# Moving closing stores, closing loads and context loads from the head of a pair to its middle in a two-layer graph kernel

## The chip, the cores and the metric

The kernel runs on one core of a Trainium2 chip. The metric is the device time of one execution in microseconds (us). A kernel is timed in several runs, and the median is taken. Besides, one execution is recorded by the hardware profiler; its page and its trace are what the readings below are taken from.

## The reference

There are 8 batches of 2048 nodes with 256 features, and one adjacency matrix. Layer 0 is a four-head attention whose softmax runs within chunks of 256 keys; layer 1 is a graph attention over all neighbours. Each has a residual sum and a layer norm. Cut to what matters:

```
# layer 0: chunked attention, then output, residual, norm
scores = einsum('bhnd,bhjcd->bhnjc', q, kc) / sqrt(64)
scores = where(mask == 0, -10, clip(scores, -10, 10))
ctx    = einsum('bhnjc,bhjcd->bhnd', softmax(scores, -1), vc)
out    = LN(ctx @ Wo.T + bo + x) * gamma + beta
x1     = LN(x + out)
# layer 1: e_ij = leaky_relu(s_src_i + s_dst_j) on the edges
Wh     = (x1 @ W).reshape(..., 4, 64)
h      = einsum('bijh,bjhd->bihd', softmax(where(adj, e, -inf), 2), Wh)
return LN(x1 + elu(h))
```

## The kernel before

All is float32. For each batch `b` the kernel runs layer 0 of `b` together with layer 1 of batch `b - 1`, and in the same loop it *closes* batch `b - 2`: it adds x1 to layer 1's result, takes the last layer norm and stores the output.

Layer 0 of a batch is a loop over 32 *pairs* (variable `p`). The queries are cut in four *quarters* `q` of 512; a quarter has 8 pairs, numbered `i` from 0 to 7: four for the first two heads and four for the other two. A pair holds two slots, `s0` and `s1`; a slot is one chunk of 256 keys for two heads. In a pair, in the order in which the code issues it:

- the head: stores that wait in a list are sent (`send`), the mask tile of the pair after the next is loaded (`load_slab`, tile `slab`), and other loads are issued; then VectorE's steps of the table `FIRST_OF` and the turn of a context tile;
- `burst(p + 1)`: the four score products (`ps`, 64 by 512, line L400) of the next pair, each evicted by VectorE with clip and mask (L417) into `pr`, and put through the exponential by ScalarE (L440). PSUM has three double banks for them, so the fourth product waits for the first eviction;
- layer 1's part: `make` builds a tile `e` on VectorE (L859) from a row (`srow`) and an edge tile (`et`), `use` multiplies it on TensorE (`pa`, L888). A pair makes and uses four tiles: two are made before the middle of the pair, two after it. Each `make` loads the edge tile that is wanted three tiles later (L805), from four buffers, so that load waits for an earlier `e`;
- the middle: VectorE's steps of `MIDDLE_OF` and `NEXT_MIDDLE`, steps of the closing, and then `product(s0)` (`pc`, L451): the slot's probabilities by the values;
- the rest: the other evictions and exponentials, more of layer 1, and `product(s1)`; at the end the steps on ScalarE, among them the closing's `finish`, which scales the output tile (L566, tile `x1g`) and puts its store (L969) on the list.

All this is an order written out by hand: every engine works through its instructions in the order of the code, and so does SP, which issues nearly all of the DMAs. An instruction of SP that waits holds those behind it.

The queries' buffer `qT` is used again for the context. When two heads of a quarter are done, ScalarE's queue stores the context to DRAM (`ctxD`, L484); `load_context` reads it back in four DMAs of 64 KB with blocks of 32 by 32 placed for the turn (L282), and `turn_context` turns it on VectorE (L495, 128 by 512) into `qT`. The output product (`po`, L602) of a quarter runs in pairs 2 and 3 of the next. The object `Between` carries a quarter from there to x1: `bias` (L586) and `shift` (L590) add the output's bias and the norm's beta to the residual `xg`, 128 by 1024.

The closing of batch `b - 2` follows the table `CLOSING`: for each pair the group of 512 nodes and the step. `load` reads x1 of a group from DRAM (L960, 512 KB), `add` adds it to layer 1's result (L963, VectorE), `sums` and `squares` run on ScalarE, `factors` on VectorE and GpSimd, `finish` as above. Batches 0 and 1 have nothing to close.

Of the kernel before, what the change touches and what calls it, by code (L numbers as in the profile page):

```python
# [21 lines left out]
def adj_resnorm_kernel(  # L22
# [47 lines left out]
    QP = QS // 2  # L70
# [134 lines left out]
    def send():  # L205
        while outgoing:
            outgoing.pop(0)()
# [285 lines left out]
    def turn_context(q, hp):  # L493

        nc.vector.transpose(qT[:, hp, q * CH : (q + 1) * CH], sums.pop((q, hp))[:, 0, :])  # L495
# [79 lines left out]
    class Between:  # L575
# [86 lines left out]
    FIRST_OF = {  # L662
        3: lambda o: o.add((0, 1)),
        4: lambda o: o.add((2, 3)),
        6: lambda o: o.shift(),
    }
    MIDDLE_OF = {
        1: lambda o: o.bias(),
        6: lambda o: o.a.factors(),
        7: lambda o: o.scale(),  # L670
    }
# [376 lines left out]
    for g in range(NCH):  # L1048
# [21 lines left out]
            finish_constants()  # L1070

    CLOSING = {
        -1: [(0, "load", HOME), (1, "load", HOME), (2, "load", HOME_Y), (3, "load", HOME_Y)],
        0: [(0, "add"), (0, "sums")],
        1: [(2, "add"), (0, "squares")],
        2: [(0, "factors"), (0, "finish")],
        3: [(1, "add"), (1, "sums")],
        4: [(1, "squares")],
        5: [(1, "factors"), (1, "finish")],
        6: [(2, "sums")],  # L1080
        7: [(3, "add"), (2, "squares")],
# [32 lines left out]
    for b in range(B):  # L1114
        waug = blocks.tile([P, NT, H, D1], F32, tag="waug", name="waug")
        sd = small.tile([P, 2 * H, NT], F32, tag="sd", name="sd", bufs=1)
        closing = Closing(b - 2, CLOSING) if b > 1 else None
        if closing:
            closing.do(-1, "load")
        group = before = None  # L1120
        for p in range(PAIRS):
            s0, s1 = 2 * p, 2 * p + 1
            q, i = p // QP, p % QP
            along = lower if b + 1 < B or s0 < SLOTS - LATE else None
            more = p + 1 < PAIRS

            def hook(now, later):
                if group and i in now:
                    now[i](group)
                if before and i in later:  # L1130
                    later[i](before)

            send()
            if p + 2 < PAIRS:
                load_slab(p + 2)
            if i == 0 and q:
                before, group = group, Between(b, q - 1, sd, waug)
            if closing:
                closing.do(p, "load")
            if i == 1 and q:  # L1140
                load_context(b, q - 1, 1)
            if i == QP // 2 + 1:
                load_context(b, q, 0)
            if p == PAIRS - 2 and b + 1 < B:
                turns = [project(b + 1, g) for g in range(NCH)]
                turns[0].pop(0)()

            hook(FIRST_OF, {})
            if i == QP - 1:
                turn_context(q, 0)  # L1150
            if p:
                normalize(s0 - 1)
            if more:
                us = units_of(p + 1)
                waiting = burst(p + 1)
                evict(*waiting[0][0], waiting[0][1])
                exps(*us[0])
                exps(*us[1])
            if along:
                along.rest(1)  # L1160
                along.make()
                along.use()
                along.make()
            else:
                if more:
                    evict(*waiting[1][0], waiting[1][1])
                    exps(*us[2])
                if not lower and masks.left():
                    masks.step()
            hook(MIDDLE_OF, NEXT_MIDDLE)  # L1170
            if closing:
                closing.do(p, "add", "factors")
            if i == 2 and q:
                turn_context(q - 1, 1)
            product(s0)
            if along:
                normalize(s0)
                if more:
                    for us_ps in waiting[1:]:
                        evict(*us_ps[0], us_ps[1])  # L1180
            elif more:
                evict(*waiting[2][0], waiting[2][1])
                exps(*us[3])
            if i == 0 and q:
                send_context(b, q - 1, 1)
            if i == QP // 2:
                send_context(b, q, 0)
            if along:
                if more:
                    exps(*us[2])  # L1190
                along.rest(1)
                along.use()
                along.make()
                along.use()
                along.make()
                along.use()
            else:
                normalize(s0)
                if not lower and masks.left() and (p < QP - 2 or p % 2 == 0):
                    masks.step()  # L1200
            if p == PAIRS - 1:
                if b + 1 < B:
                    turns[0].pop(0)()
                group.again()
            product(s1)
            if along and more:
                exps(*us[3])
            hook(LAST_OF, NEXT_LAST)
            hook(FINALLY_OF, NEXT_FINALLY)
            if closing:  # L1210
                closing.do(p, "sums", "squares", "finish")
        normalize(SLOTS - 1)

        send()
        before = group
        gd, fs = factors(b, sd, waug)
        group = None

        def begin():
            nonlocal group  # L1220
            group = Between(b, NCH - 1, sd, waug)

        def ctx():
            context(NCH - 1, 1)

        coming = Layer1(b, gd, waug)
        spare.clear()

        parts = WHOLE if b + 1 < B else HALVES

        def start_next():
            for us, ps in burst(0):
                evict(*us, ps)

        early = [
            lambda: before.b2.stats(every),
            lambda: None,
            lambda: before.finish(),
            lambda: before.load(ep.tile([P, KC, CH], F32, tag="e", name="x1t") if b + 1 < B else None),
            lambda: before.turn(),  # L1240
            lambda: before.values((0, 1), parts),
            lambda: before.values((2, 3), parts),
        ]

        steps = [
            lambda: group.bias(),
            lambda: group.output(every, parts),
            lambda: group.add(every),
            lambda: (group.shift(), group.a.stats(every)),
            lambda: group.a.apply(group.y),  # L1250
            lambda: (group.scale(), group.again(), group.b2.stats(every)),
            lambda: group.finish(),
            lambda: group.turn_all(),
            lambda: group.values((0, 1), parts),
            lambda: group.values((2, 3), parts),
        ]
        if b + 1 < B:
            (k0, v0, q0), (l1, t1, k1, v1, q1), (l2, t2, k2, v2, q2), (l3, t3, k3, v3, q3) = turns
            rest = [lambda: lower.rest(1)] if lower else []
            order = [begin, early[0], *rest, l1, k0, ctx, early[2], v0, steps[0], *rest, steps[1], t1, l2, *rest]  # L1260
            order += [q0, steps[2], early[3], steps[3], l3, k1, *rest, steps[4], v1, early[4], t2, q1]
            order += [steps[5], k2, steps[6], early[5], early[6], steps[7], coming.begin, v2, t3]
            order += [lambda: [load_slab(p) for p in range(2)], steps[8], steps[9]]
            order += [lambda: k3(fs[0]), fs[1], lambda: q2(fs[2]), coming.start, v3, start_next]
            order += [lambda: [exps(*us) for us in units_of(0)], q3, coming.make, coming.make]
        else:

            step = lower.step
            order = [begin, early[0], lambda: coming.load_half(0, 0), step, ctx, early[1], step, steps[0], steps[1], early[2], step]
            order += [steps[2], step, steps[3], early[3], step, steps[4], step, steps[5], early[4], step]  # L1270
            order += [steps[6], early[5], step, steps[7], early[6], step, steps[8], step, steps[9], step]
            order += [fs[0], step, fs[1], step, fs[2], coming.start]
            order += [step] * 5
            assert sum(p is step for p in order) == LATE
        for piece in order:
            send()
            piece()
        send()
        undone = lower.tail if lower else []
        lower = coming  # L1280
        if b + 1 == B:
            lower.begin()
        lower.tail += undone
# [57 lines left out]
```

## Time and profile before

| | |
|---|---|
| median of the three timed runs | 3684.75 us (3678.33 to 3687.97) |
| the profiled execution | 3676.19 us |
| its span, first to last instruction | 3674.4 us |
| granted TensorE clock, mean | 0.991 |
| DMA traffic | 512.33 MB, 139 GB/s |
| eviction L417 (128 x 1024), mean of one | 1205 ns, 960 of them |
| `e` L859 (128 x 1024), mean of one | 1335 ns, 896 of them |
| closing store L969, `out_dram<-x1g` | 24, 512 KB each, 3.3 us from issue to landing |
| x1 load L960, `x1g<-x1D` | 24, 512 KB each, 6.1 us to landing |
| context load L282, `ctx<-ctxD` | 224, 64 KB each, 3.8 us to landing |
| mask tile L388 and edge tile L805 | 256 and 896, 256 KB each, 4.2 and 3.3 us to landing |

Busy times on the page are unions of the instructions' times, with the share of the span. In a row of a timeline stand the start, the time from the first instruction's start to the last one's end, the engine, the line, the operation and tiles, how many were merged, and in brackets the idle time before it with what ended it. PE is TensorE's matrix products, PEld its weight loads, SPq the queue of SP. In the list of waits a row has the total in us, the number of times and the longest. "Issue" is idle time in which the engine waited for nothing that the profile shows.

### The profile page before, as it was taken

How to read it: one execution, taken by the hardware profiler on the slowest of the kernel's cores; microseconds unless marked ns; L12 is line 12 of the kernel's file. 1: busy time of each engine (PE TensorE's matmuls, PEld its weight loads, DVE VectorE, ACT ScalarE, POOL GpSimd, SP SyncE). 2: the span in 40 equal slices, each digit the busy share in tenths (PEclk: the TensorE clock that was granted, in tenths of full speed). 3: DMA queues.
4: the chain of work that ended last, by engine and by line, in shares of the span. 5: the costliest groups of instructions: out<-in, count | busy, mean ns of one | idle time of the engine just before them, and what ended most of it. 6: DMA issues, size and time to landing. Idle time of an engine off the chain costs nothing. (4 is left out here: it accounts for less than half of the span.)

```text
span 3674.4 us, 169302 instructions
## 1 busy us (share of the span) xinstructions
PE 3529.9 (96%) x76884; PEld 2627.9 (72%) x76884; DVE 3043.1 (83%) x3652; ACT 2302.7 (63%) x4119; POOL 1437.2 (39%) x1259
## 2 busy tenths in 40 slices
PE   8999999999999999999999999999999999998777
PEld 5666677777777677776777767777677776775677
DVE  5886689968899698995999959998789977896787
ACT  5786556656666566665666656665566655666376
POOL 1555333333333333333433424334234333334376
PEclk9999999999999999999999999999999999999898
DMA  7754344545555455554555545555455554543432
GB/s 192 174 131 94 109 141 144 147 116 159 153 143 145 101 166 152 149 149 116 149 152 144 136 135 163 146 149 125 135 152 149 152 125 143 152 144 94 142 129 83
DMA packets 692866, 512.33 MB, mean 139 GB/s; under 512 B 429616, under 2 KB 528304, under 8 KB 692144
## 3 DMA queue, kind: packets, MB, share of 16 engines
q1 hardware_dynamic: 642144, 467.80, 46.0%
q10 hardware_dynamic: 50000, 33.70, 2.9%
q8 instruction: 601, 9.85, 1.1%
q14 instruction: 121, 0.99, 0.1%
HBM read 440.27 MB, written 61.08 MB: 136 GB/s over the span
## 5 line engine op out<-in xcount | busy, mean ns | idle before, releaser
L440 ACT ACTIVATE pr<-pr 128x1024 f32<-128x1024 f32 x960 | 997.8, 1054 | 445.3 <-DVE pr L417 371.9
L417 DVE SCALAR_TENSOR_TENSOR pr<-ps,slab 128x1024 f32<-128x1024 f32 x960 | 1117.5, 1205 | 118.3 <-PE ps L400 95.3
L859 DVE SCALAR_TENSOR_TENSOR e<-srow,gd,et 128x1024 f32<-128x1024 f32 x896 | 1168.3, 1335 | 25.3 <-PE pa L888 9.5
L888 PEld LDWEIGHTS pa<-waug,e 128*64 128x64 f32 x32768 | 1015.1, 140 | 233.3 <-issue 184.5
L888 PE MATMUL pa<-waug,e 128*64 128x65 f32 x32768 | 1069.2, 225 | 54.7 <-DVE e L859 30.6
L451 PE MATMUL pc<-vaug,pr 128*64 128x65 f32 x30720 | 989.4, 222 | 35.5 <-issue 25.4
L451 PEld LDWEIGHTS pc<-vaug,pr 128*64 128x64 f32 x30720 | 943.2, 138 | 57.6 <-issue 29.1
L475 POOL TENSOR_TENSOR part<-raw,rd 128x512 f32<-128x512 f32 x448 | 477.5, 1066 | 1282.3 <-DVE rd L468 1277.9
L400 PE MATMUL ps<-qT,kT 64*64 64x512 f32 x8192 | 950.3, 597 | 14.3 <-DVE pr L417 13.2
L458 ACT COPY raw<-pc 128x520 f32<-128x520 f32 x512 | 302.6, 591 | 553.2 <-PE pc L451 550.7
L400 PEld LDWEIGHTS ps<-qT,kT 64*64 64x64 f32 x8192 | 289.4, 132 | 497.4 <-issue 272.7
L477 POOL TENSOR_TENSOR acc<-acc,part 128x512 f32<-128x512 f32 x448 | 587.1, 1311 | 35.2
L468 DVE RECIPROCAL rd<-raw 128x8 f32<-128x8 f32 x512 | 100.7, 197 | 176.8 <-ACT raw L458 167.7
L475 POOL TENSOR_TENSOR acc<-raw,rd 128x512 f32<-128x512 f32 x64 | 66.8, 1043 | 362.2 <-DVE rd L468 362.2
L644 PE MATMUL pw<-w_sb,x1T 128*64 128x264 f32 (+1 forms) x800 | 124.7, 391 | 4.8 <-DVE x1T L300 4.7
L344 PE MATMUL pp<-xT,wk_sb 128*128 128x512 f32 x256 | 118.4, 602 | 2.9 <-DVE xT L300 1.6
L602 PE MATMUL po<-wo_sb,qT 128*64 128x256 f32 (+1 forms) x912 | 120.2, 379 | 0.0
L344 PE MATMUL pp<-xT,wq_sb 128*128 128x512 f32 x256 | 117.4, 598 | 0.0
L924 ACT ACTIVATE sums<-sums,dn 128x64 f32<-128x64 f32 x448 | 117.1, 334 | 0.4 <-ACT y L566 0.4
L360 PE MATMUL pv<-wv_sb,xT 128*128 128x256 f32 x512 | 116.6, 381 | 0.0
L360 PEld LDWEIGHTS pv<-wv_sb,xT 128*128 128x128 f32 x512 | 95.9, 190 | 20.2 <-issue 7.2
L830 POOL TENSOR_TENSOR e<-e,et 128x1024 f32<-128x1024 f32 x42 | 90.0, 2146 | 48.4 <-ACT e L829 41.1
(140 smaller groups left out, 2525.1 us busy)
## 6 DMA issues: line engine op xcount, KB each, us to landing
et<-edgeD SPq DMA_DIRECT2D x896, 256.0 KB, 3.3
slab<-clipD SPq DMA_DIRECT2D x256, 256.0 KB, 4.2
srow<-rowD SPq DMA_DIRECT2D x64, 512.0 KB, 4.9
xg<-in_x_dram SPq DMA_DIRECT2D x32, 512.0 KB, 5.4
x1D<-y ACTq DMA_DIRECT2D x32, 512.0 KB, 2.9
ctxD<-acc ACTq DMA_DIRECT2D x56, 256.0 KB, 3.7
ctx<-ctxD SPq DMA_DIRECT2D x224, 64.0 KB, 3.8
xp<-in_x_dram SPq DMA_DIRECT2D x224, 64.0 KB, 2.4
```

The costliest lines, as they stand in the source:

```text
L344: nc.tensor.matmul(pps[c], lhsT=w[:, kc, c * P : (c + 1) * P], rhs=st["xT"][:, kc, :], start=(kc == 0), stop=(kc == KC - 1),)
L360: nc.tensor.matmul(pv[:, u, :], lhsT=st["xT"][:, kc, u * P : (u + 1) * P], rhs=wv_sb[:, kc, :], start=(kc == 0), stop=(kc == KC - 1),)
L400: nc.tensor.matmul(ps[z * D : (z + 1) * D, k, :], lhsT=kT[rows, hp, t * P + z * D : t * P + (z + 1) * D], rhs=qT[rows, hp, cols], start=Tr ...
L417: nc.vector.scalar_tensor_tensor(pr, ps, -CLIP, row.unsqueeze(1).to_broadcast([P, 2, CH]), op0=ALU.max, op1=ALU.min,)
L440: nc.scalar.activation(pr, pr, AF.Exp, scale=0.125)
L451: nc.tensor.matmul(pc[z * D : (z + 1) * D, k, to], lhsT=probs[s][u][:, k, i * P + z * D : i * P + (z + 1) * D], rhs=vaug[:, KT * c + u, 2 ...
L458: nc.scalar.copy(raws[s].rearrange("p k i d -> p k (i d)"), pc[:, :, : QT * D1])
L475: nc.gpsimd.tensor_mul(part, raw[:, :, :, :D], rd.to_broadcast([P, 2, QT, D]))
L477: nc.gpsimd.tensor_add(accv, accv, part)
L644: nc.tensor.matmul(pw[z, k, : F + 2 * H], lhsT=self.x1T[:, c, u * P + z.start : u * P + z.stop], rhs=w1_sb[:, c, :], start=(c == 0), stop= ...
L859: nc.vector.scalar_tensor_tensor(e, row, self.gd[:, h, j : j + 1], self.mask(k), op0=ALU.max, op1=ALU.mult,)
L888: nc.tensor.matmul(self.pa[i // QT][z * D : (z + 1) * D, i % QT, :], lhsT=e[:, i * P + z * D : i * P + (z + 1) * D], rhs=self.waug[:, j, h ...
```

## The change

Four things are put elsewhere; no operation is added or left out.

- `send()`, the closing's loads and both `load_context` calls go from the head of the pair to behind `product(s0)`. The load of the mask tile and of `xg` stay at the head.
- The four x1 loads of the closing, which were all issued ahead of pair 0, are spread: group 0 ahead of pair 0, groups 1, 2 and 3 in pairs 0, 2 and 4. The addition for group 2 goes from pair 1 to pair 4.
- `shift` of group 0 goes from the head of pair 14 (`i` = 6 of quarter 1) to the middle of pair 13; for the other groups it stays.
- `turn_context(q, 0)` of quarters 0 and 1 goes from the head of pairs 7 and 15 to the middle of pairs 6 and 14; for quarters 2 and 3 it stays.

```diff
     FIRST_OF = {
         3: lambda o: o.add((0, 1)),
         4: lambda o: o.add((2, 3)),
-        6: lambda o: o.shift(),
+        6: lambda o: o.g != 0 and o.shift(),
     }
     MIDDLE_OF = {
         1: lambda o: o.bias(),
+        5: lambda o: o.g == 0 and o.shift(),
         6: lambda o: o.a.factors(),
         7: lambda o: o.scale(),
     }
...
     CLOSING = {
-        -1: [(0, "load", HOME), (1, "load", HOME), (2, "load", HOME_Y), (3, "load", HOME_Y)],
-        0: [(0, "add"), (0, "sums")],
-        1: [(2, "add"), (0, "squares")],
-        2: [(0, "factors"), (0, "finish")],
+        -1: [(0, "load", HOME)],
+        0: [(1, "load", HOME), (0, "add"), (0, "sums")],
+        1: [(0, "squares")],
+        2: [(2, "load", HOME_Y), (0, "factors"), (0, "finish")],
         3: [(1, "add"), (1, "sums")],
-        4: [(1, "squares")],
+        4: [(3, "load", HOME_Y), (2, "add"), (1, "squares")],
         5: [(1, "factors"), (1, "finish")],
...
-            send()
             if p + 2 < PAIRS:
                 load_slab(p + 2)
             if i == 0 and q:
                 before, group = group, Between(b, q - 1, sd, waug)
-            if closing:
-                closing.do(p, "load")
-            if i == 1 and q:
-                load_context(b, q - 1, 1)
-            if i == QP // 2 + 1:
-                load_context(b, q, 0)
...
             hook(FIRST_OF, {})
-            if i == QP - 1:
+            if i == QP - 1 and q > 1:
                 turn_context(q, 0)
...
             if i == 2 and q:
                 turn_context(q - 1, 1)
+            if i == QP - 2 and q < 2:
+                turn_context(q, 0)
             product(s0)
+            send()
+            if closing:
+                closing.do(p, "load")
+            if i == 1 and q:
+                load_context(b, q - 1, 1)
+            if i == QP // 2 + 1:
+                load_context(b, q, 0)
```

## The prediction

> **What bounds the kernel now.** I read the page's busy times first, then TensorE's waits, then the timeline of TensorE pair by pair, and for each gap found there the timelines of SP and VectorE. The page:
>
> ```profile
> PE 3529.9 (96%) x76884; PEld 2627.9 (72%) x76884; DVE 3043.1 (83%) x3652; ACT 2302.7 (63%) x4119; POOL 1437.2 (39%) x1259
> ...
> q8 instruction: 601, 9.85, 1.1%
> ```
>
> TensorE is busy 96% of the span. So the change, which touches no matrix product, can only win back what TensorE loses. The order of the instructions on PE, ACT and POOL is the same in both kernels; only those of DVE and SP differ.
>
> The second line matters more than its 1.1% tells. 9.85 MB in 601 packets is 16.4 KB each, and 2 x 76,884 TensorE instructions over 601 is 256. Queue 8 is TensorE's own instruction stream, in blocks of 256. Its waits:
>
> ```profile
> PE pa L888 <- DVE e L859: 30.6, 16, 4.6
> PE pc L451 <- issue: 26.3, 27, 2.6
> PE pa L888 <- issue: 20.6, 17, 2.3
> PE ps L400 <- DVE pr L417: 13.2, 22, 2.0
> ```
>
> The first row is nearly all in the stages between and after the pairs, which the change leaves alone. The rows to look at are "issue" (46.9 us) and "ps <- DVE pr". Reading the starts of the score products (ps) of successive pairs, an undisturbed pair takes 11.21 us, 12.94 with an output product and 12.99 with layer 1's values. Summing what pairs take beyond this over batches 1 to 7 (up to pair 22 in the last, where the stage changes) gives 75 us: 6.5 in batch 1, which closes nothing, and 9 to 14 in each of batches 2 to 7, which do. That is all there is to win here.
>
> Two kinds of gap make it up. The first, in pair 3 of batch 2 (TensorE, then SP):
>
> ```profile
> 874.26 3.66 PE L400 MATMUL ps<-qT,kT 64*64 64x512 f32 x32
> ...
> 883.51 0.28 PE L451 MATMUL pc<-vaug,pr 128*64 128x65 f32 x2
> 884.93 2.08 PE L451 MATMUL pc<-vaug,pr 128*64 128x65 f32 x62 [1.14 <-issue]
> ```
>
> ```profile
> 877.97 0.39 SPq L969 DMA_DIRECT2D out_dram<-x1g  x1
> 878.41 0.50 SPq L388 DMA_DIRECT2D slab<-clipD  x1
> 879.00 7.06 SPq L805 DMA_DIRECT2D et<-edgeD  x4
> ```
>
> The product stops after 2 of 64 matmuls, in the middle of work whose operands are all there: no semaphore ends such a gap. Counting TensorE's instructions, each of the 40 "issue" gaps over 0.25 us in the trace stands at the same place modulo 256 (193 or 194). They are waits for the next block of instructions. The packets of queue 8 show the rest: when one block begins, the packet for the next starts 0.2 to 0.6 us later if the DMA queues are idle, but 2.7 us later here (crossing at 879.78, packet at 882.49) and up to 3.6 us in pair 6, and TensorE goes on 2.3 to 2.4 us after the packet's start. A block with no score products lasts 3.73 us, so it tolerates 1.4 us of delay and the rest is a stall. Here the closing store had stood before the slab and the edge loads: SP was held by it until ScalarE had finished the tile (877.97), and then four transfers went out together just ahead of the request. Pair 0 of batch 2 is worse:
>
> ```profile
> 838.71 2.08 SPq L960 DMA_DIRECT2D x1g<-x1D  x4
> ...
> 841.50 8.60 SPq L805 DMA_DIRECT2D et<-edgeD  x4
> ```
>
> ```profile
> 848.90 1.09 PE L888 MATMUL pa<-waug,e 128*64 128x65 f32 x29 [1.73 <-issue]
> ```
>
> Four loads of 512 KB, 2 MB, go out in 2.1 us, and the block asked for at 843.16 starts to arrive at 846.47.
>
> The second kind is VectorE at the start of a pair (batch 1, pairs 13 to 15; VectorE, then TensorE):
>
> ```profile
> 560.79 0.20 DVE L468 RECIPROCAL rd<-raw 128x8 f32<-128x8 f32 x1 [1.26 <-ACT raw L458]
> ...
> 565.75 1.21 DVE L590 TENSOR_TENSOR xg<-xg,beta_sb 128x1024 f32<-128x1024 f32 x1
> ...
> 578.59 0.70 DVE L495 STREAM_TRANSPOSE qT<-ctx 128x512 f32<-128x512 f32 x1
> ```
>
> ```profile
> 568.23 1.09 PE L400 MATMUL ps<-qT,kT 64*64 64x512 f32 x8 [0.76 <-DVE pr L417]
> ...
> 580.53 1.09 PE L400 MATMUL ps<-qT,kT 64*64 64x512 f32 x8 [0.85 <-DVE pr L417]
> ```
>
> The addition of beta and the turn stand ahead of the first eviction, whose PSUM tile the fourth score product needs. Yet in the middle of pair 13 VectorE sits idle for 1.26 us, waiting for the first product.
>
> **What the Trainium skill says.** "Runtime: NRT & Kernel Launch", section Instruction fetch mechanics: instructions come in 16 KiB blocks of 256, through a DMA queue of the engine's own, and crossing a block's border is "mostly hidden". The trace agrees on the block; on the hiding it agrees only where the queues are idle. "DMA: Bandwidth & Descriptors", section Issuing engines are not separate DMA queues: all transfers run on the same 16 engines and interleave. The delays above agree that a fetch stands behind data already queued.
>
> **The change, part by part.** The sum is against the profiled execution, 3676.2 us (span 3674.4); the median of the three timed runs is 8.6 us above, and I carry the difference over to it.
>
> The place "after product(s0)" means for SP: after the pair's second edge load, which waits for the pair's first e. So what is moved leaves SP about 4.3 us into the pair, where before it stood at the head, ahead of the slab and all four edge loads.
>
> 1. Four x1 loads at once become one at the head and one each in the middle of pairs 0, 2 and 4. Pair 0 exceeds its length by 13.2 us in six batches (1.4 to 3.7). The trace's landings are 1.5 to 2.3 us apart for such loads; with two gone and one sent 5 us before the other, a request at about 4.6 us finds at most one in front, 1.9 us, against a tolerance of 1.4: half a microsecond each, 3 in all. Gain 10. Pairs 2 and 4 receive 12 loads that they did not have: if a quarter of them meets a short block at 0.7 us, 2 lost. Bounds 0 and 12 x 0.7 = 8.
>
> 2. The 24 closing stores. Pairs 3, 6, 9 and 12 exceed by 20.1 us (13 of 24 show an "issue" gap, 14.9 us together, about 0.2 us more each in the pair's length). In the middle, ScalarE's tile is long ready, slab and first edge load have gone out with the pair's start, and slab and one edge load (0.65 to 1.2 us apart in landing) no longer stand between store and request: about 1.4 us less delay on gaps of 1.15 on average. But the store goes out nearer the request than the head's items do, so a third stays. Gain 13, bounds 5 and 18. With it goes a second effect: the edge tile that came late in pair 9 (the 1.58 us "DVE e <- DMA et" wait of batch 2, where store and context loads held SP) and delayed pair 10, 3.75 us in six batches. Gain 3.
>
> 3. Context loads, four of 64 KB, in the middle of pairs 1 and 5 of a quarter. These pairs lose 15.0 us now, and there it is the row load (512 KB) and the third edge load, issued after the second, that stand before the request. Four context loads take SP 2.0 us and land 0.2 to 0.3 us apart, 1.2 us of the queues: they push row and edge behind the early requests, and lengthen the queue for late ones. I take 6 gained; bounds +12 and -10. The row is wanted a pair or two later and the edge tile four tiles later, so SP's 2 us are covered; the turn comes a pair after the load, some 10 us, against 3.8 us to landing.
>
> 4. VectorE. Beta for group 0 (1.21 us) goes to the middle of pair 13 where 1.26 us are idle; the turn (0.70) goes to the middle of pairs 6 and 14. Pairs 14 and 15 exceed by 11.5 us over seven batches, pair 7 by 0.9 in batches 1 to 6. Pair 14 keeps 9.6 us of evictions and e, 0.9 of layer 1's closing, 0.3 of factors and now 0.7 of turn, 11.5 against 11.21, so about 0.3 stays per batch, with some in pair 15. Gain 9.5. Nothing is queued behind the turn but the second product's evictions, which have a product's time.
>
> 5. The second addition of x1 (1.22 us) moves from the middle of pair 1 to that of pair 4, where 1.16 us are idle in the place of 1.2 in pair 1: nothing. Batch 0, where the slab now goes ahead of the mask stores, is not held by TensorE or by slabs: nothing, give or take 2 us.
>
> Sum: 10 - 2 + 13 + 3 + 6 + 9.5 = 39.5, so 40 us: the profiled execution becomes about 3636, the median 3684.75 - 40 = 3645.
>
> **The rivals.** *The fetches wait elsewhere* (0.22): the moved transfers go out just where short blocks ask for their successor, and what pairs 3, 6 and 9 lose stays. For it: the request ahead of such a block comes 4 to 8 us into the pair in four cases of five, and 4.3 lies in that window. Against: fewer bytes stand in the queue there. Then items 4 and the late edges remain (12.5) with half of item 1 (5): 3667.
>
> *All gaps go* (0.08): the store and the context loads are too short to be seen, and 60 of the 75 us vanish: 3625.
>
> *Slower* (0.08): the same window, at its full price. 89 transfers or sets of them are moved (47 context sets, 24 stores, 18 loads). If each one that meets a short block costs 1.4 us (a stall of 1.2, and 0.2 of restart), then 44 of them use up all that parts 1, 2, 3 and 4 remove (48 of fetch stalls with their restarts, 13 of VectorE's). At two in three, 59, it is 83 against 61: 3707. It decides from one in two; before, 35 of 237 blocks shorter than 4.6 us stalled, so that would need the middle to be far worse than the head.
>
> *VectorE becomes the bound* is inside the forecast: its work in an ordinary pair is 9.6 us of 11.21.
>
> **How the numbers follow.** Forecast 0.62 (gain 28 to 52: 3633 to 3657), and the cases above. About 0.3%, 11 us, is what a measurement of this kernel can tell from no change. Faster: 0.62 + 0.08 + most of 0.22 = 0.87; within it 0.07; slower 0.06. The range takes in the rival at 3667 and the one at 3625, 3622 to 3674.
>
> **What would show it.** Right: pair 0 at 11.2 to 12 us in batches 2 to 7; pairs 14 and 15 within 0.5 of 11.21; the two "issue" rows below 25 us together; no "DVE e <- DMA et" over 1 us in pair 9; SP's closing stores without a wait for ScalarE. Wrong: "issue" gaps at pairs 2, 4, 5 or 9 as long as those gone, VectorE late at the start of pairs 7 or 15 still, or a lower granted clock that gives the won time back.

## The result and the profile after

The changed kernel takes 3635.42 us (median of 4 runs, 3633.24 to 3639.75) against 3683.26 us of the kernel before in the same group (four runs; the table further up has three of them): ratio 0.9874, 95% interval 0.9858 to 0.9890, 48 us less. The profiled execution went from 3676.2 to 3633.6 us, its span from 3674.4 to 3631.8. The forecast was 3645 for the median and about 3636 for the profiled execution.

The page's busy times:

```profile
PE 3523.5 (97%) x76884; PEld 2627.0 (72%) x76884; DVE 3040.0 (84%) x3652; ACT 2301.9 (63%) x4119; POOL 1434.6 (40%) x1259
```

The engines do the same work (TensorE 3529.9 us before); it is packed more closely. TensorE's waits (total in us, times, longest):

```profile
PE pc L451 <- issue: 10.5, 20, 1.3
...
PE pa L889 <- issue: 9.0, 10, 2.1
...
PE ps L400 <- DVE pr L417: 4.1, 6, 2.8
```

"Issue" fell from 46.9 to 19.5 us, the wait for VectorE's evictions from 13.2 to 4.1.

Pair 0 of batch 2, SP and then TensorE:

```profile
838.94 0.43 SPq L961 DMA_DIRECT2D x1g<-x1D  x1
839.48 0.45 SPq L388 DMA_DIRECT2D slab<-clipD  x1
839.97 4.50 SPq L806 DMA_DIRECT2D et<-edgeD  x2
844.51 0.59 SPq L961 DMA_DIRECT2D x1g<-x1D  x1
```

```profile
838.81 3.66 PE L400 MATMUL ps<-qT,kT 64*64 64x512 f32 x32
...
850.02 3.67 PE L400 MATMUL ps<-qT,kT 64*64 64x512 f32 x32
```

One x1 load where four stood, another 5.7 us into the pair, and the next pair begins after 11.21 us instead of 13.26. In pair 3 the store now waits for nobody: it leaves SP 5.1 us after the pair's first score product, behind slab and two edge loads, and the pair takes 11.21 us:

```profile
873.77 4.84 SPq L806 DMA_DIRECT2D et<-edgeD  x2
878.66 0.43 SPq L970 DMA_DIRECT2D out_dram<-x1g  x1
```

```profile
873.56 3.67 PE L400 MATMUL ps<-qT,kT 64*64 64x512 f32 x32
...
884.77 3.81 PE L400 MATMUL ps<-qT,kT 64*64 64x512 f32 x32
```

The same read on VectorE in pairs 13 and 14 of batch 1, and on TensorE at the start of pairs 14, 15 and 16:

```profile
560.92 1.22 DVE L590 TENSOR_TENSOR xg<-xg,beta_sb 128x1024 f32<-128x1024 f32 x1
...
572.96 0.70 DVE L495 STREAM_TRANSPOSE qT<-ctx 128x512 f32<-128x512 f32 x1
```

```profile
566.24 3.66 PE L400 MATMUL ps<-qT,kT 64*64 64x512 f32 x32
...
577.45 3.88 PE L400 MATMUL ps<-qT,kT 64*64 64x512 f32 x32
...
588.88 3.66 PE L400 MATMUL ps<-qT,kT 64*64 64x512 f32 x32
```

The score products are no longer broken in the middle: pair 14 takes 11.21 us and pair 15 11.43, where they took 12.20 and 12.29 (counted from row to row).

Part of the fetch stalls moved to where the transfers went. Pair 2 of batch 2, which had none, has one now, with the x1 load of group 2 in its middle:

```profile
872.48 1.15 PE L451 MATMUL pc<-vaug,pr 128*64 128x65 f32 x30 [0.59 <-issue]
```

The table holds what the pairs take beyond 11.21, 12.94 or 12.99 us, summed over batches 1 to 7 (to pair 22 in the last) and read from the timelines. It has the experiments too; "row" pairs are 5, 13, 17 and 25, four of the seven where layer 1's row load and context loads meet (9 stands in another column, 21 and 29 under "rest").

| kernel (us) | pair 0 | 2, 4 | 3, 6, 9, 12 | 10 | row pairs | 14, 15 | 8, 16, 24 | rest | all |
|---|---|---|---|---|---|---|---|---|---|
| before | 13.2 | 0.2 | 20.9 | 3.7 | 12.7 | 11.5 | 5.5 | 7.2 | 74.9 |
| changed | 0.7 | 4.2 | 6.6 | 1.4 | 4.2 | 2.1 | 5.7 | 6.0 | 30.9 |
| changed, again | 0.2 | 4.9 | 4.6 | 1.2 | 3.1 | 2.2 | 5.4 | 5.5 | 27.1 |
| e1, VectorE only | 11.7 | 1.2 | 15.4 | 5.4 | 11.0 | 1.6 | 5.4 | 7.2 | 58.9 |
| e2, x1 only | 1.0 | 3.5 | 15.0 | 4.6 | 15.1 | 10.9 | 4.9 | 7.9 | 63.0 |
| e3, stores only | 14.6 | 0.5 | 6.9 | 1.8 | 11.8 | 11.8 | 7.0 | 9.0 | 63.3 |
| e4, context only | 14.3 | 1.0 | 20.4 | 6.0 | 1.2 | 14.5 | 6.3 | 4.3 | 68.0 |
| e9, all transfers | 1.2 | 4.6 | 4.7 | 1.6 | 3.1 | 14.4 | 6.8 | 8.4 | 44.7 |
| e5, head, not held | 0.0 | 2.1 | 2.6 | 1.4 | 2.0 | 2.1 | 6.6 | 7.1 | 23.8 |
| e6, row at the head | 1.3 | 7.4 | 7.0 | 1.0 | 4.2 | 2.1 | 5.0 | 9.0 | 37.0 |
| e7, both | 0.0 | 3.2 | 9.1 | 12.5 | 1.5 | 3.0 | 8.4 | 8.2 | 46.0 |
| e10, third make | 0.0 | 1.7 | 14.7 | 4.6 | 9.2 | 1.6 | 8.1 | 11.6 | 51.6 |
| e11, halves | 0.0 | 3.9 | 4.4 | 1.0 | 12.9 | 0.7 | 1.5 | 5.2 | 29.7 |

The 44 us that left the table, less 3 us lost in batch 0 and plus about 2 won in the stages outside it, are the 42.6 us of the span. Batch 1's first score product stands at 393 us in the kernel before (and in e8, its shifted copy) and between 395 and 400 us in the others, e2 included, which changes nothing in batch 0; that is left open.

The granted clock has a share. An undisturbed pair takes 11.21 us in both traces. But in the trace of the kernel before the granted clock fell to 0.50 twice within these pairs, for 3.4 us each (at 1739.9 and 3135.9 us), and in the changed kernel's never. One such fall costs about 1.7 us: pair 7 of batch 7, which holds the second and no stall of its own, takes 12.91 us. So some 3 of the 44 us are the clock's. The falls go with the stalls: all nine within the pairs of all traces (two before, one each in e3 and e4, three in e7, two in e10) begin between 0.2 us before and 1.3 us after the end of an "issue" gap of 1.8 to 2.9 us. Thirteen gaps of that length have none, so what decides it is not shown.

### The profile page after: what moved, and what is told of

It is laid out like the page before. It is cut to its first block, busy times and chain, and to the rows that moved or that the text cites. A ratio compares the mean times of both kernels' runs of the same rounds, so it can differ in the third digit from the quotient of the medians.

```text
span 3631.8 us, 169340 instructions
## 1 busy us (share of the span) xinstructions
PE 3523.5 (97%) x76884; PEld 2627.0 (72%) x76884; DVE 3040.0 (84%) x3652; ACT 2301.9 (63%) x4119; POOL 1434.6 (40%) x1259
## 4 chain that ended last, share of the span: by engine, by line
PE 86%; DVE 6%; issue 3%; ACT 2%; POOL 2%; DMA 1%; SPq 0%; DVEq 0%; ACTq 0%; POOLq 0%
PE pc L451 24%; PE ps L400 23%; PE pa L889 23%; PE pp L344 6%; PE po L602 3%; PE pv L360 3%; PE pw L644 3%; DVE e L860 2%; DVE pr L417 2%; POOL acc L477 1%; POOL part L475 1%; DMA et<-edgeD 0%; PE pm L249 0%; DVE h L417 0%; ACT e L829 0%
## 5 line engine op out<-in xcount | busy, mean ns | idle before, releaser
L860 DVE SCALAR_TENSOR_TENSOR e<-srow,gd,et 128x1024 f32<-128x1024 f32 x896 | 1166.8, 1335 | 17.8 <-PE pa L889 10.9
L889 PE MATMUL pa<-waug,e 128*64 128x65 f32 x32768 | 1066.7, 225 | 42.2 <-DVE e L860 30.2
```

The source lines that it names most:

```text
L860: nc.vector.scalar_tensor_tensor(e, row, self.gd[:, h, j : j + 1], self.mask(k), op0=ALU.max, op1=ALU.mult,)
L889: nc.tensor.matmul(self.pa[i // QT][z * D : (z + 1) * D, i % QT, :], lhsT=e[:, i * P + z * D : i * P + (z + 1) * D], rhs=self.waug[:, j, h ...
```

## The experiments

Kernels of one group ran on one chip beside the kernel before. Its median was 3683 us with the result, and 3674, 3682, 3680 and 3671 us in the four groups below, so a time is compared through its ratio within its group. Each row of the table is one profiled execution, and columns that an experiment doesn't touch show how far one can be trusted: where the stores stay at the head (e1, e2, e4) pairs 3, 6, 9 and 12 lose 15.0 to 20.4 us, and where the x1 loads stay (e1, e3, e4) pair 0 loses 11.7 to 14.6.

### The four parts alone (first group)

e1 takes the changes of the two tables and of `turn_context`, e2 those of `CLOSING` and of its loads, e3 that of `send`, e4 that of `load_context`; each alone on the kernel before:

```diff
 # e1
-        6: lambda o: o.shift(),
+        6: lambda o: o.g != 0 and o.shift(),
...
+        5: lambda o: o.g == 0 and o.shift(),
...
-            if i == QP - 1:
+            if i == QP - 1 and q > 1:
                 turn_context(q, 0)
...
+            if i == QP - 2 and q < 2:
+                turn_context(q, 0)
 # e2: the changed CLOSING, and
             product(s0)
+            if closing:
+                closing.do(p, "load")
 # e3
             product(s0)
+            send()
 # e4
             product(s0)
+            if i == 1 and q:
+                load_context(b, q - 1, 1)
+            if i == QP // 2 + 1:
+                load_context(b, q, 0)
```

> Only VectorE's two steps are moved (beta of group 0 to pair 13, the turns of two quarters to pairs 6 and 14); all DMAs stay at the head. Theory F (TensorE waits for its next block of instructions behind queued transfers, and apart from that for VectorE at the head of pairs 14 and 15): pairs 14 and 15 fall from 1.0 us each over 11.21 to 0.4 together, the issue gaps stay at about 38 us, and the gain is 8 to 10 us. Rival S (all gain comes from SP being held at the head, which makes edge tiles and evictions late): under 3 us.

> Only the closing's x1 loads are spread and put in the middle (with the second addition in pair 4). Theory F: pair 0 of batches 2 to 7 falls from 2.2 us over its length to under 0.5, pairs 2 and 4 gain up to 0.3 each, and the gain is 8 to 12 us; pairs 3, 6, 9 and 12 keep their gaps. Rival S: the x1 loads never wait on SP for anything, so under 3 us.

> Only send() is put behind product(s0). Theory F: pairs 3, 6, 9, 12 and the pair after 9 lose 15 to 20 of their 24 us; pair 0 keeps its 2.2 us per batch. Rival S: nearly the whole gain of the change except VectorE's part, 30 us or more.

> Only the context loads are put behind product(s0). Theory F: pairs 5, 13, 17 and 25 lose half of their 15 us because row and third edge load now stand behind the context loads and so behind early requests for instructions: gain 3 to 9 us, most of it in pairs 13 and 17. Rival M (the middle is itself a bad place, and what the context loads lose there is hidden by the other moves): 3 to 8 us slower.

Measured against 3674.4 us: e1 0.9975 (0.9965 to 0.9985), 9 us; e2 0.9977 (0.9967 to 0.9988), 8 us; e3 0.9985 (0.9977 to 0.9993), 6 us; e4 0.9986 (0.998 to 0.9993), 5 us. TensorE's waits in e1:

```profile
PE pc L451 <- issue: 20.2, 28, 1.8
PE pa L889 <- issue: 18.9, 18, 2.0
...
PE ps L400 <- DVE pr L417: 7.1, 10, 2.4
```

VectorE's part halves the last row, and pairs 14 and 15 go from 11.5 to 1.6 us, about its whole gain in time: theory F. (The two "issue" rows are 39.1 us together against 46.9, though no transfer was moved; that is within the spread of the untouched columns.) e2 empties pair 0 (13.2 to 1.0) and leaves the rest, though no x1 load ever held SP: rival S, which gave it under 3 us, falls. e4 empties the row pairs (12.7 to 1.2), so M falls too. e3 takes 15.9 us from pairs 3, 6, 9, 12 and 10, as F had it, and leaves pair 0; yet its time fell by only 6 us, far from the 30 of S.

The sizes don't close in the times: the four gains are 28 us together, against 48 of the whole. In the table they come to 16.0 + 11.9 + 11.6 + 6.9 = 46.4 against 44.0, in the spans of the profiled executions to 38 against 43: batch 0 was 1 to 4 us longer in each of the four, most in e3. But both sums count every part from the one trace of the kernel before, on the chip of the result. On the chip of the parts that kernel was 9 us faster, and its trace there doesn't exist, so whether it had fewer stalls to lose was not seen. That the parts simply add up is therefore not shown.

### The whole again, and other places (second group)

e5 is the changed kernel with stores and x1 loads back at the head, but one at a time and without holding SP; e6 moves layer 1's row load to the head of the next pair; e7 is both.

```diff
 # e5
+            send()
+            outgoing.extend(ready)
+            ready.clear()
             if p + 2 < PAIRS:
                 load_slab(p + 2)
+            if closing:
+                closing.do(p, "load")
...
-            outgoing.append(lambda: nc.sync.dma_start(out=by_node(out, self.b, self.g), in_=o))
+            (outgoing if self.alone else ready).append(
+                lambda: nc.sync.dma_start(out=by_node(out, self.b, self.g), in_=o)
+            )
...
+        1: [(1, "load", HOME), (0, "squares")],
+        3: [(2, "load", HOME_Y), (1, "add"), (1, "sums")],
+        6: [(3, "load", HOME_Y), (2, "sums")],
 # e6
-            if j == NT // 2:
+            if j == (NT // 2 if self.alone else NT // 2 + 2):
                 self.load_row(n + 1)
```

> The changed kernel once more, beside the kernel before on the chip of this group. The four parts alone gained 0.25, 0.23, 0.15 and 0.14%, 0.77% together, the whole 1.26% on another chip. If the parts add up and the difference lies between the chips: ratio 0.992 to 0.993 here. If they help one another (a request that two causes delay is late while either is left): 0.987 to 0.988.

> The changed kernel, but closing stores and x1 loads go out at the head again, one at a time: x1 of groups 1, 2 and 3 at the head of pairs 1, 3 and 6, and each store one pair later, when ScalarE has long finished its tile, so that SP is never held. Theory F says that what counts is how much stands in the queue 4 to 8 us into a pair: sent at the head's place, 1 us ahead of the pair, 512 KB are through by then, so the gaps in pairs 2, 3, 4, 6 and 12 shrink below those of the changed kernel, 3 to 8 us faster than it. Rival P (the middle is the right place as such, because slab and edge loads go first): 5 us or more slower than the changed kernel.

> The changed kernel with layer 1's row load (512 KB, every fourth pair) issued in the first make of the next pair instead of the third make of pairs 1, 5, 9 and so on, that is at the head instead of at 5 us. Theory F: pairs 1, 5, 9, 13, 17, 21 and 25 lose most of their 9.5 us of excess, gain 5 to 9 us over the changed kernel. Rival: the row load does no harm there, the context loads do: under 2 us.

> Both: closing at the head without being held, and the row load at the head. Theory F: 8 to 15 us faster than the changed kernel. Rival: the head is then full where row, store or x1 load meet (pairs 6 and 10), and new gaps of 1 to 2 us take half of it back.

Against 3682.4 us: the whole 0.9878 (0.9863 to 0.9893), 3635.5 us; e5 0.9854 (0.9841 to 0.9867), 3628.6 us (3626.8 to 3630.3, below every run of the changed kernel); e6 0.988 (0.9867 to 0.9893), 3638.1; e7 0.9909 (0.9895 to 0.9923), 3648.9.

The whole gave the same ratio as with the result. By what was expected, 0.992 or more would have meant that the parts add up and this that they help one another; but it was again not the chip of the parts, so a difference between chips stays a rival.

e5 beats both kernels, so the middle is not what makes the change good. TensorE's waits in e5:

```profile
PE pa L889 <- issue: 13.7, 16, 2.6
...
PE pc L451 <- issue: 3.2, 9, 0.6
```

Pairs 3, 6, 9 and 12 are down to 2.6 us. e6 was a miss. The pairs that the row load left (1, 5, 9, 13, 17, 21 and 25) still lose 7.0 us, against 8.5 and 5.9 in the two traces of the changed kernel, as the rival had it; those that it came to (2, 6, 10 and so on to 26) went from 5.3 and 5.7 to 14.2. e7's rival named pairs 6 and 10, which now lose 7.9 and 12.5 us; here it is in pair 10 of batch 4 (SP, then TensorE), where a store, slab and row, 1.25 MB, stand together:

```profile
1831.02 0.39 SPq L971 DMA_DIRECT2D out_dram<-x1g  x1
1831.46 0.50 SPq L388 DMA_DIRECT2D slab<-clipD  x1
1832.01 0.92 SPq L791 DMA_DIRECT2D srow<-rowD  x1
```

```profile
1840.67 2.54 PE L889 MATMUL pa<-waug,e 128*64 128x65 f32 x41 [2.15 <-issue]
```

It cost more than the half that the rival gave it: e7 is slower than either of its parts. Three falls of the clock, in pairs 6 and 10, make some 5 of the 46.0 us that its row of the table has; one begins where the gap above ends.

### Blocks shifted, transfers together, and the third make (third group)

e8 is the kernel before with 64 more TensorE instructions in front; e9 is the changed kernel without VectorE's part; e10 issues the moved transfers later still (`issue` holds the calls that had moved behind `product(s0)`).

```diff
 # e8
+    for _ in range(4):
+        pj = two_banks([P, 2, CH], "pj")
+        for k in range(8):
+            nc.tensor.transpose(pj[:, k // 4, k % 4 * P : (k % 4 + 1) * P], identf, identf)
 # e10
                 along.use()
                 along.make()
+                issue(p, i, q)
                 along.use()
                 along.make()
```

> The kernel before with 32 idle transposes (64 TensorE instructions, a quarter of a block) put in before the first product, whose result nobody reads; nothing else is changed. Theory F: the issue gaps over 0.25 us still stand at 193 or 194 modulo 256 counted from the program's start, so each has moved by 64 instructions against the work around it, to other products of the pair; their sum stays between 25 and 50 us, and the time within 10 us of before. Rival D (they are waits for data or buffers that the trace does not name): they stay at the same places of the work, and so stand at 1 or 2 modulo 256.

> All three moves of transfers, VectorE's two steps as before. If the parts add up: 20 us faster than before (8.5 + 5.5 + 5, from the runs of each alone), and the changed kernel is 9 us faster still. If the moves of transfers help one another: 30 us or more faster than before, ratio below 0.992.

> The changed kernel with the moved stores, x1 loads and context loads issued behind the third make instead of behind product(s0), so that on SP they follow the third edge load, at about 7 us into the pair where SP is idle. Theory F: most requests for instructions (4 to 8 us) are then ahead of them, so pairs 2, 3, 4, 9, 12 and 13 lose their gaps: 5 to 12 us faster than the changed kernel, as fast as the head without being held or faster. Rival: late requests now meet them, and what is left comes from the edge, row and xg loads, which stay: within 4 us of the changed kernel.

Against 3680.5 us: e8 0.9991 (0.9981 to 1.0002); e9 0.9915 (0.99 to 0.993), 3648.5 us; e10 0.9927 (0.991 to 0.9944), 3655.6 us.

e8 decides what the gaps are. All 50 "issue" gaps over 0.25 us stand at 193 or 194 modulo 256 again, counted from the start of a program that is 64 instructions longer. Pair 0 of batch 2 shows it in the work:

```profile
847.48 1.16 PE L893 MATMUL pa<-waug,e 128*64 128x65 f32 x33
850.19 2.02 PE L893 MATMUL pa<-waug,e 128*64 128x65 f32 x62 [1.55 <-issue]
```

The pause comes after 33 matmuls of this run where it came after 66: 33 matmuls with their weight loads earlier, the 64 instructions to within two. A wait for data would have stayed where it was. D falls.

e9 kept VectorE's gaps and no more, 14.4 us in pairs 14 and 15, and "ps <- DVE" is its largest row of the three:

```profile
PE ps L400 <- DVE pr L417: 15.4, 24, 2.9
...
PE pa L888 <- issue: 10.4, 10, 2.4
PE pc L451 <- issue: 10.3, 24, 1.0
```

It is 32 us faster than before, not the 20 of the parts' times, which by the expectation means that the moves help one another. The table has 30.2 us for it and 11.9 + 11.6 + 6.9 = 30.4 for the three parts, which would mean that they add up. As the parts were not run on this chip, it stays open.

e10 was a miss: 20 us slower than the changed kernel. Behind the third make the context loads follow row and edge at once (pair 5 of batch 7, SP, then TensorE):

```profile
3096.70 1.05 SPq L791 DMA_DIRECT2D srow<-rowD  x1
3097.85 0.39 SPq L806 DMA_DIRECT2D et<-edgeD  x1
3098.33 2.92 SPq L282 DMA_DIRECT2D ctx<-ctxD  x4
```

```profile
3106.66 4.31 PE L400 MATMUL ps<-qT,kT 64*64 64x512 f32 x24 [2.89 <-issue]
```

The block was asked for at 3098.97, with row, edge and the first two context loads just issued, and its packet started 5.3 us later. The block that ran meanwhile holds 6 of a pair's 32 score matmuls and lasts 4.8 us without the stall, so it tolerates 2.4 us of delay where a block with none tolerates 1.4. Even that was not enough: 7 of e10's 32 stalls hit blocks with score products, none in the kernel before and one in the changed kernel. (The gap falls at the start of pair 6, which has 12.1 of the 14.7 us under 3, 6, 9 and 12.) The moved transfers left SP 6.6 us into the pair (median), and this request came at 7.5: late requests met them, as the rival said, which gave it only 4 us.

### Halves (fourth group)

On e5, the row load and the load of `xg` are cut in two, and x1 of group 1 goes to the head of pair 2.

```diff
+            if j == NT // 2 - 2 and not self.alone:
+                self.load_row(n + 1, (0,))
             if j == NT // 2:
-                self.load_row(n + 1)
+                self.load_row(n + 1, (0, 1) if self.alone else (1,))
...
             product(s0)
+            if i == 0 and q:
+                group.load_half(1)
```

> Built on the kernel with the closing at the head and SP not held (ratio 0.9854 to before): layer 1's row load and the load of xg are each cut into two of 256 KB that go out half a pair apart (row: first and third make of pairs 1, 5, 9 and so on; xg: head and middle of pairs 8, 16 and 24), and x1 of group 1 moves from the head of pair 1 to that of pair 2. Theory F, as the runs so far leave it (there is no free place; a request is late by what stands in the queue at that moment, and 1.4 us are free): a half is about 0.9 us and seldom makes a request late, so pairs 1, 8, 16, 17 and 24 lose most of their 12 us over the length, and it is 4 to 9 us faster than that kernel, ratio 0.983 to 0.9845. Rival (the number of transfers counts, or the head is too full where half a row meets a store, pair 13): ratio 0.9854 or above.

3634.6 us against 3670.8: 0.9905 (0.9889 to 0.9922). It did not reach e5's ratio of 0.9854, as the rival had it, which had named pair 13 (the two ratios are from two chips). Where it aimed it worked: pairs 8, 16 and 24 fell from 6.6 to 1.5 us. But pair 13 alone takes 8.8 us more than its length; a store, slab, half a row, two edges, the context and the other half stand there (batch 5, SP, then TensorE):

```profile
2297.39 0.51 SPq L982 DMA_DIRECT2D out_dram<-x1g  x1
2297.95 0.50 SPq L388 DMA_DIRECT2D slab<-clipD  x1
2298.49 1.06 SPq L800 DMA_DIRECT2D srow<-rowD  x1
2299.65 2.65 SPq L815 DMA_DIRECT2D et<-edgeD  x2
2302.39 2.98 SPq L282 DMA_DIRECT2D ctx<-ctxD  x4
```

```profile
2308.33 0.62 PE L900 MATMUL pa<-waug,e 128*64 128x65 f32 x14 [2.09 <-issue]
```

A version with that store elsewhere was not tried.

## Why the prediction held, point by point

The cause and the sign were right, and the forecast of 3645 was 10 us too high. Most of that is not in the parts: the profiled execution was forecast at 3636 and took 3633.6. The prediction added the 8.6 us by which the median before lay above its profiled execution, and the changed kernel's lies only 1.8 us above. That the profiled executions agree so closely is in part luck: the parts gave some 5 us more than was taken, and batch 0 lost 3, which was put at nothing, give or take 2. By the prediction's own parts, from the table and the two traces:

- Part 1, x1 loads: pair 0 gave 12.5 us where 10 were taken, pairs 2 and 4 took 4.0 where 2 were. Net 8.5 against 8, and e2's time says 8. About 1 us of the 12.5 is the fall of the clock in batch 4.
- Part 2, stores: in the batches that close, pairs 3, 6, 9 and 12 gave 14 us against 13, pair 10 2.3 against 3. The sum agrees better than a single trace can tell (with the stores unmoved, these pairs differ by 5 us between traces), and e3's time says only 6. The waits of SP for ScalarE's closing tile (L969 for `x1g`: 84 us in 24 waits) are gone from the list, and the longest "DVE e <- DMA et" is 0.4 us.
- Part 3, context loads: this is the mis-sized term. 6 us were taken, between +12 and -10; the context pairs gave 10 (15.0 to 4.8, with pair 29 and batch 1's pair 9; pair 21, left out of this, went from 0.8 to 1.6). The reason stands as given: row and edge go behind the early requests. The row load left SP 5.2 us into its pair before and leaves it at 7.5 now (medians). e4 shows the row pairs at 1.2 us with this move alone. That late requests would suffer was what held the estimate down, and in the middle of these pairs they hardly did; e10 shows that they do when the same loads come 1.5 us later, with the row load ahead of them again.
- Part 4, VectorE: pairs 14, 15 and 7 gave 9.8 us against 9.5, and what stays in pair 15 is 0.3 a batch, as worked out. e1 says 9.
- Part 5, the second addition: nothing was taken for it. What pairs 2 and 4 lose is in "issue" gaps; no gap of TensorE over 0.25 us in pair 4 of the changed kernel is a wait for VectorE.

The place was worked out too early: what was moved leaves SP 5.1 us into the pair or later (median 5.3), not 4.3, and a store, which ScalarE had held until 3.7 us before, came only some 1.6 us later. It now stands behind slab and two edge loads, which is what the part on the stores counted on.

The rivals: "the fetches wait elsewhere" is there in small, in pairs 2 and 4; one gap in pair 4, 1.26 us in batch 5, is as long as the mean of the 13 gaps of pairs 3, 6, 9 and 12 before (14.9 us), so that sign of being wrong came once. The slower one did not come about at this place, but its mechanism is what e7 and e10 ran into.

One thing in the argument was too simple. It spoke of less delay for the fetches. Over the 464 blocks of the pairs, the time from request to packet is 1.0 us in the mean in both kernels, and some 115 requests are over 1.4 us late in both. What fell is the number that are over 3 us late, 18 to 7, and among the 207 blocks without score products, the short ones, 11 to none; the stalls over 0.25 us went from 35 to 21. The transfers are the same and make as many fetches late; they were parted so that the long delays no longer meet the short blocks. That a packet waits behind data is read from what SP had issued; the trace doesn't tell which DMA engine carries a packet, so the place where it waits is not shown.

## What to carry to other kernels

A gap of a saturated engine that ends in the middle of a run of equal instructions, with no semaphore, is worth counting in instructions: if such gaps stand at one place modulo 256, the engine waits for its program, and what to look at is what the DMA queues hold some microseconds earlier. Here it was not the total of the transfers that cost, which is the same in both kernels, but 1 to 2 MB issued within a few us around a request. So part them, try a place where a store needn't wait for its producer at the head of an in-order queue, and expect that a move frees one pair and may fill another. The two steps of VectorE ahead of the first eviction (1.21 and 0.70 us) cost TensorE 0.99 and 1.08 us in pairs 14 and 15 of batch 1; half a pair earlier, where VectorE was idle, they left 0.0 and 0.2 there.

## What the hardware showed that was not expected

With 1 MB issued from 2.3 us before a request to 2.3 us after it, an instruction packet of 16 KB started 5.3 us late, although it runs in a queue of its own. Some waits for instructions cost more than their own length: 9 of the 22 that lasted 1.8 us or more, in all traces, went with 3.4 us at a granted clock of 0.50. And transfers moved to SP's idle time, 6.6 us into the pair, made the kernel 20 us slower than in the middle (3655.6 against 3635.5 us, in two groups whose kernel before differed by 2 us).
